# Moving bias adds, residual adds and PSUM evictions from VectorE to TensorE and ScalarE in a graph network kernel

## The chip, the cores and the metric

The kernel runs on one core of a Trainium2 chip. A core has TensorE (PE in the profile, with its weight loads listed apart as PEld), VectorE (DVE), ScalarE (ACT), GpSimd (POOL), and SyncE (SP), which issues DMAs here. Each engine executes its own instructions in program order, and engines wait for each other through semaphores. The metric is the time of one execution on the device in microseconds (us). The kernel before took 5338.34 us, the median of four runs that lie between 5337.52 and 5340.61 us.

## The reference

There are 16 graphs of 1024 nodes with 64 features each, and a weighted adjacency of 1024 x 1024 per graph. Four layers follow each other; each has the form x = layernorm(x + f(x, adj)).

```python
# layer 0
messages = einsum('bij,bjh->bih', adj, x)
f0 = tanh(concat([x, messages]) @ W1 + b1) @ W2 + b2
# layer 1
f1 = (adj / clip(sum(adj, axis=2), 1)) @ x
# layers 2 and 3, each with its own weights
adj_d = dilate(adj, mask)            # drops some neighbours of nodes with more than 10 of them
agg = 0.25*q(0.25) + 0.5*q(0.5) + 0.25*q(0.75)   # quantiles over each node's neighbours, per feature
f23 = (relu((x + agg) @ W1 + b1) @ W2 + b2) * mask
```

The quantiles need the neighbours' features in sorted order, for every node and feature. All arithmetic is float32 in and out.

## The kernel before

**Tiling.** A graph's features stand as eight tiles of 128 nodes x 64 features (NT = 8), and most steps work on halves of four tiles (G = 4, NH = 2). Nodes are ordered by their number of neighbours, so that tile t holds nodes with at most SIZES[t] of 10, 11, 13, 14, 15, 17, 19 and 33 members each. For tiles 0 to 6, POOL gathers the neighbours' rows from DRAM with indirect DMAs into a ring of ROOM slots in SBUF (`got_s`, line 352). For tile 7, with the longest lists, TensorE picks the rows by matmuls with one-hot matrices: VectorE writes a one-hot tile `hot` for each list position, and 24 matmuls (line 348) take the features, split into three bf16 parts, into PSUM (`pgk`), from where ScalarE copies them to `got` (line 727). The generator `fill` does this, 32 positions for each of two graphs, with `HOTS` = 4 buffers for `hot`. VectorE then sorts every list by a network of minima and maxima (`other`, `got_s`, `got`), ScalarE weighs the wanted order statistics (`weigh`, line 737), and VectorE sums them into `agg`.

**Rounds.** The main loop runs `sort_round(k)` for 18 rounds. Round k sorts layer 2 of graph k together with layer 3 of graph k-2. It sorts tiles 6 to 0, then calls `weave.finish(filling)`, which emits what is left of `fill`, and then sorts tile 7.

**The order of the work.** Everything besides the sorting is written as generators: `features` (layers 0 and 1 of a graph), `lists` and `ordered` (neighbour lists and their order), `fill`, `weigh`, and `finish` (the two small matrix products and the layernorm of layers 2 and 3). A planner, `Weave`, interleaves them with the sorting. Its clock is VectorE's estimated work, which the wrapper `Metered` adds up at 0.13 us plus one element a lane per cycle of 960 MHz. A generator yields the number of us after which it is due again, and `catch_up`, called after each sorting instruction, runs those that are due. `finish` and `advance` skip the clock forward when there is no sorting left to emit. The program order on VectorE, ScalarE and TensorE is the order in which these generators are run. The DMA queues of SP and POOL are filled by the same code.

**What the change touches.**

- `features`, layer 0: two halves. For each, TensorE transposes the own features and multiplies with the adjacency (`px`, lines 416 and 420), applies W1 (line 429), ScalarE takes tanh, and TensorE applies W2 into `pd` (line 436). After `yield 10`, VectorE adds `pd` and the own features x_s into y. After both halves VectorE adds the bias row b02r, which had been broadcast to 128 partitions. Then `settle` does the layernorm.
- `features`, layer 1: two halves. TensorE multiplies the adjacency with x1 and a column of ones (`pa`, line 451); VectorE makes the degree's reciprocal and multiplies `pa` by it into y. After both halves VectorE adds x1, and `settle` follows. Both `px`, `pd` and `pa` share one PSUM buffer (tag "x"). The flag `e.near`, for which `lists` polls, is set behind the second half.
- `finish`: VectorE adds the features xc to `agg`. For each half, TensorE transposes `agg` into `pt` (line 758), ScalarE copies it out, TensorE applies W1 (`ph`, line 764), ScalarE takes relu, and TensorE applies W2 into `pd` (line 771). After `yield 9` VectorE adds `pd` and the broadcast bias. After both halves VectorE multiplies by the mask, adds xc, and `settle` follows. `pt`, `ph` and `pd` share one PSUM buffer (tag "m").
- A second path for lists that are too long for the rounds (`layer0`, `layer1`, `mlp` at the end of the file) lies in a branch that these inputs do not take.

## Time and profile before

| | |
|---|---|
| median of four runs | 5338.34 us |
| the profiled execution's own time | 5337.5 us |
| its span, first to last instruction | 5335.7 us |
| mean granted TensorE clock | 0.732 |
| DVE busy | 4689.2 us in 9407 instructions |
| PE busy / PEld busy | 3428.3 us / 2656.0 us |
| POOL busy | 3658.9 us in 3228 instructions |
| ACT busy | 1969.3 us in 4644 instructions |

A row such as "L348 PE MATMUL pgk<-x3p,hot 128*128 128x64 bf16 x12288 | 597.7, 218 | 320.3 <-DVE hot L207 302.5" names the line, engine and operation, what is written from what, the shape and the count. Then come the busy time of the whole group, the mean ns of one instruction, and the idle time of the engine just before such instructions with what ended it. Line 207 is the wrapper through which every VectorE instruction of the rounds passes, so its instructions are told apart by their tiles. An f32 matmul with ordinary weights leaves two records, an f32 transpose leaves one: the 128 matmuls of line 436 are 256 records.

### The profile page before, as it was taken

What the parts mean: (1) busy time and instruction counts of PE and PEld (TensorE: products, weight loads), DVE (VectorE), ACT (ScalarE), POOL (GpSimd) and SP (SyncE); (2) the same over time, 40 slices, a digit from 0 to 9 for tenths busy, and PEclk for the clock granted to TensorE, in tenths of its full rate; (3) what the DMA queues carried; (4) which work ended last, traced back from release to release, by engine and by line L of the source; (5) the groups of instructions that cost most, each with busy time, mean ns of one, the idle gap of its engine ahead of it and who ended that gap; (6) DMA issues with size and microseconds to landing.
All of it is one profiled execution on the core that took longest, in us unless ns stands there. A gap on an engine that the chain in (4) does not pass through costs nothing.

```text
span 5335.7 us, 106955 instructions
## 1 busy us (share of the span) xinstructions
PE 3428.3 (64%) x43073; PEld 2656.0 (50%) x43144; DVE 4689.2 (88%) x9407; ACT 1969.3 (37%) x4644; POOL 3658.9 (69%) x3228
## 2 busy tenths in 40 slices
PE   6766477667585857858584867748576774625332
PEld 5645355455373645646363655636364563524222
DVE  2685779998999999999999989899898989999977
ACT  3351435243443525352524335342533534212111
POOL 0426547777678787787777776777678776787572
PEclk7877688678686968777787868777786866656555
DMA  3312122212122222222121222212122220111010
GB/s 87 76 39 60 31 59 58 69 42 55 41 59 57 58 57 56 60 54 61 37 73 35 50 58 52 63 40 70 31 50 58 54 48 18 28 22 26 15 24 10
DMA packets 420585, 259.11 MB, mean 49 GB/s; under 512 B 106590, under 2 KB 368878, under 8 KB 420078
## 3 DMA queue, kind: packets, MB, share of 16 engines
q0 software_dynamic: 102400, 105.06, 10.6%
q1 hardware_dynamic: 317678, 147.12, 10.0%
q8 instruction: 339, 5.55, 0.4%
q14 instruction: 168, 1.38, 0.1%
HBM read 239.37 MB, written 12.58 MB: 47 GB/s over the span
## 4 chain that ended last, share of the span: by engine, by line
DVE 66%; PE 14%; issue 8%; POOL 5%; DMA 3%; ACT 3%; SPq 0%; DVEq 0%; POOLq 0%; ACTq 0%
DVE other L207 21%; DVE got_s L207 15%; DVE got L207 9%; DVE hot L207 5%; POOL got_s L352 4%; DVE best L207 4%; PE pgk L348 4%; PE pk L592 3%; DMA got_s<-table,idx 3%; PE pa L451 2%; DVE less L207 2%; PE px L420 2%; DVE y_x L207 1%; PE pr L506 1%; DVE y_m L207 1%
## 5 line engine op out<-in xcount | busy, mean ns | idle before, releaser
L352 POOL DMA_INDIRECT got_s<-table,idx x2944 | 3363.7, 1143 | 1470.3 <-issue 775.1
L348 PEld LDWEIGHTS <-hot 128*128 128x128 bf16 x24576 | 1025.0, 112 | 707.3 <-DVE hot L207 629.5
L348 PE MATMUL pgk<-x3p,hot 128*128 128x64 bf16 x12288 | 597.7, 218 | 320.3 <-DVE hot L207 302.5
L348 PE MATMUL pgk<-x2p,hot 128*128 128x64 bf16 x12288 | 531.6, 208 | 228.1 <-DVE hot L207 219.5
L207 DVE TENSOR_TENSOR other<-got_s 128x512 f32<-128x512 f32 (+8 forms) x900 | 515.1, 584 | 47.4 <-DMA got_s<-table,idx 35.1
L737 ACT ACTIVATE got_s<-got_s,wts 128x64 f32<-128x64 f32 x1568 | 399.6, 335 | 355.5 <-DVE got_s L207 354.7
L207 DVE TENSOR_TENSOR got_s<-got_s 128x384 f32<-128x384 f32 (+7 forms) x918 | 491.1, 537 | 18.8
L207 DVE TENSOR_SCALAR hot<-place 128x1024 bf16<-128x1024 f16 x1024 | 448.5, 440 | 45.6 <-PE pgk L348 45.1
L592 PE MATMUL pk<-near,order 128*128 128x512 f16 x2048 | 475.4, 386 | 13.4 <-DVE order L207 8.0
L549 PE MATMUL pv<-minus_n,takes 128*128 128x128 bf16 x1024 | 230.6, 253 | 385.7 <-DVE takes L207 385.2
L506 PE MATMUL pr<-steps,near 128*128 128x512 bf16 x1465 | 382.6, 413 | 129.5 <-ACT junk L512 87.2
L451 PE MATMUL pa<-x,adj_r 128*128 128x65 f32 x2048 | 395.7, 375 | 92.0 <-DMA adj_r<-in_adj_dram 32.2
L451 PEld LDWEIGHTS pa<-x,adj_r 128*128 128x128 f32 x2048 | 383.2, 289 | 96.6 <-issue 37.8
L207 DVE TENSOR_TENSOR got_s<-other 128x512 f32<-128x512 f32 (+8 forms) x774 | 409.1, 541 | 7.2
L549 PEld LDWEIGHTS <-takes 128*128 128x128 bf16 x1024 | 116.0, 113 | 558.8 <-DVE takes L207 409.1
L207 DVE TENSOR_TENSOR other<-other 128x128 f32<-128x128 f32 (+13 forms) x558 | 318.8, 571 | 14.8
L548 PE MATMUL pv<-scaled,near 128*128 128x128 f16 x1024 | 231.5, 254 | 146.3 <-ACT near L553 146.2
L207 DVE TENSOR_TENSOR other<-got 128x128 f32<-128x128 f32 (+5 forms) x270 | 233.3, 881 | 103.6 <-ACT got L727 101.1
L506 PEld LDWEIGHTS <-near 128*128 128x128 f16 x1536 | 157.3, 105 | 328.3 <-issue 192.6
L592 PEld LDWEIGHTS <-order 128*128 128x128 bf16 x2048 | 195.7, 99 | 243.7 <-issue 23.3
L512 ACT ACTIVATE junk<-pr,nb_st 128x1024 f16<-128x1024 f32 x256 | 282.2, 1109 | 25.7 <-PE pr L506 25.0
L420 PE MATMUL px<-adj_r,x_s 128*64 128x128 f32 x2048 | 283.8, 299 | 10.6 <-DMA adj_r<-in_adj_dram 7.0
(195 smaller groups left out, 6268.4 us busy)
## 6 DMA issues: line engine op xcount, KB each, us to landing
adj_r<-in_adj_dram SPq DMA_DIRECT2D x256, 512.0 KB
got_s<-table,idx POOLq DMA_INDIRECT x2944
x_s<-in_x_dram SPq DMA_DIRECT2D x16, 256.0 KB
table<-x SPq DMA_DIRECT2D x16, 256.0 KB
x<-table SPq DMA_DIRECT2D x16, 256.0 KB
table<-x3s,rows POOLq DMA_INDIRECT x128
out_dram<-agg,out_rows POOLq DMA_INDIRECT x128
table<-no_row SPq DMA_DIRECT2D x6, 0.2 KB
```

What stands on the lines that cost most here:

```text
L207: return call(*args, **kwargs)
L348: nc.tensor.matmul(dst, hot[:, c, :], parts[:, c, q, :], start=first and c + q == 0, stop=c == NT - 1 and q == 2)
L352: nc.gpsimd.indirect_dma_start(out=dst, out_offset=None, in_=tab, in_offset=bass.IndirectOffsetOnAxis(ap=rows, axis=0))
L420: nc.tensor.matmul(px[C:, q * P : (q + 1) * P], x_s[:, jt, :], adj[t][:, jt, :], start=jt == 0, stop=jt == NT - 1)
L451: nc.tensor.matmul(pa[:, q, :], adj[i][:, jt, :], x1[:, jt, :], start=jt == 0, stop=jt == NT - 1)
L506: nc.tensor.matmul(pr[:, h * HALF : (h + 1) * HALF], near[:, c, t * P : (t + 1) * P], steps[:, ONSET + h * HALF - c * P :][:, :HALF], star ...
L512: nc.scalar.activation(junk, prs[t - 1], AF.Sign, bias=lim[:, i, t - 1 : t], scale=-1.0, accum_out=cut_at[:, i, t - 1 : t])
L548: nc.tensor.matmul(pv[:, cols], near[:, c, rows], scaled[:, c, :], start=True, stop=False)
L549: nc.tensor.matmul(pv[:, cols], takes[:, c, rows], minus_n, start=False, stop=False)
L592: nc.tensor.matmul(cols, order[:, c, t * P : (t + 1) * P], left(c, slice(h * G, (h + 1) * G)), start=c == 0, stop=c == NT - 1)
L737: nc.scalar.activation(prods[:, m, i, :], got[:, m, slot_id, :], AF.Copy, scale=e.wts[:, t, i : i + 1])
```

## The change

In layer 0, two more f32 matmuls follow each W2 matmul into the same PSUM columns: a one-row matmul of ones with the bias row, and the identity with the own features. ScalarE copies the finished sum to y. In layer 1, ScalarE takes `pa` out tile by tile with the reciprocal degree as its per-partition scale. In `finish`, xc and `agg` are both multiplied with the identity into `pt`, which adds and transposes them, the bias comes by a one-row matmul, and ScalarE takes `pd` out tile by tile with the mask as its scale. The broadcast bias tiles are replaced by three one-row tiles and a row of ones; the ring of gathered rows has 75 slots in place of 76. Several yields of the planner are added. The second path makes its own broadcast of the bias.

```diff
-ROOM = 76
+ROOM = 75
...
-    w01s, b01c, w02s, b02r = weight(w01, "w01s"), column(b01, "b01c"), weight(w02, "w02s"), per_row(b02, "b02r")
+    w01s, b01c, w02s = weight(w01, "w01s"), column(b01, "b01c"), weight(w02, "w02s")
...
+    bias_rows = [row(b, f"bias_row{i}") for i, b in enumerate((b02, b22, b32))]
+    ones_row = const.tile([1, P], F32, name="ones_row")
+    nc.vector.memset(ones_row, 1.0)
...
# features, layer 0
             for q in range(G):
-                nc.tensor.matmul(pd[:, q, :], hid_t[:, q * P : (q + 1) * P], w02s, start=True, stop=True)
+                nc.tensor.matmul(pd[:, q, :], hid_t[:, q * P : (q + 1) * P], w02s, start=True, stop=False)
+                nc.tensor.matmul(pd[:, q, :], ones_row, bias_rows[0], start=False, stop=False)
+                nc.tensor.matmul(pd[:, q, :], ident, x_s[:, h * G + q, :], start=False, stop=True)
             yield 10
-            dve.tensor_add(y[:, h * G : (h + 1) * G], pd, x_s[:, h * G : (h + 1) * G])
-        dve.tensor_add(y, y, b02r[:, None, :].to_broadcast([P, NT, C]))
+            nc.scalar.copy(y[:, h * G : (h + 1) * G], pd)
+        yield 4
...
# features, layer 1
-            dve.tensor_mul(y[:, h * G : (h + 1) * G], pa[:, :, :C], deg[:, 1, :, None].to_broadcast([P, G, C]))
+            yield 1
+            for q in range(G):
+                nc.scalar.activation(y[:, h * G + q, :], pa[:, q, :C], AF.Copy, scale=deg[:, 1, q : q + 1])
+        yield 5
         e.near = near
...
# finish
-        dve.tensor_add(agg, agg, xc)
         for h in range(NH):
             pt = s.psum.tile([P, HALF], F32, name="pt", tag="m", bufs=1)
             for q in range(G):
-                nc.tensor.transpose(pt[:C, q * P : (q + 1) * P], agg[:, h * G + q, :], ident)
+                nc.tensor.matmul(pt[:C, q * P : (q + 1) * P], xc[:, h * G + q, :], ident, start=True, stop=False)
+                nc.tensor.matmul(pt[:C, q * P : (q + 1) * P], agg[:, h * G + q, :], ident, start=False, stop=True)
...
             for q in range(G):
-                nc.tensor.matmul(pd[:, q, :], h_t[:, q * P : (q + 1) * P], w2s, start=True, stop=True)
+                nc.tensor.matmul(pd[:, q, :], h_t[:, q * P : (q + 1) * P], w2s, start=True, stop=False)
+                nc.tensor.matmul(pd[:, q, :], ones_row, bias_rows[1 + layer], start=False, stop=True)
             yield 9
-            dve.tensor_add(y[:, h * G : (h + 1) * G], pd, b2r[:, None, :].to_broadcast([P, G, C]))
-        dve.tensor_mul(y, y, e.mask[:, :, None].to_broadcast([P, NT, C]))
+            for t in range(h * G, (h + 1) * G):
+                nc.scalar.activation(y[:, t, :], pd[:, t - h * G, :], AF.Copy, scale=e.mask[:, t : t + 1])
+        yield 4
         dve.tensor_add(y, y, xc)
```

## The prediction

> **What bounds the kernel now.** I read the page's busy shares first, then the waits of VectorE, then one round in stretches, then VectorE's timeline where that round's fill ends.
>
> ```profile
> PE 3428.3 (64%) x43073; PEld 2656.0 (50%) x43144; DVE 4689.2 (88%) x9407; ACT 1969.3 (37%) x4644; POOL 3658.9 (69%) x3228
> ...
> DVE 66%; PE 14%; issue 8%; POOL 5%; DMA 3%; ACT 3%; SPq 0%; DVEq 0%; POOLq 0%; ACTq 0%
> ```
>
> VectorE is the busiest engine and holds two thirds of the chain that ended last. Its 646 us of idle time lie mostly at the start: it is busy 449 of the first 750 us.
>
> ```profile
> DVE other L207 <- ACT got L727: 101.1, 14, 10.7
> DVE y_x L207 <- PE pd L436: 58.5, 5, 20.0
> DVE hot L207 <- PE pgk L348: 45.1, 38, 4.3
> ```
>
> These are VectorE's three longest waits (total, times, longest). The second, which the change touches, falls in the first 750 us whole. The first comes once a round, where tile 7's sort waits for the last copy of the fill. One late round has these stretches (busy PE, PEld, DVE, ACT, POOL, then the granted clock):
>
> ```profile
> 3246.00:3300.00 54.00, 43.46 (x594) 33.88 (x595) 52.92 (x115) 25.69 (x61) 42.47 (x37) 0.81 0.27 61
> 3300.00:3350.00 50.00, 48.81 (x704) 33.27 (x702) 47.00 (x81) 18.92 (x36) 38.12 (x40) 1.00 0.21 49
> 3350.00:3400.00 50.00, 35.38 (x369) 32.30 (x370) 46.99 (x112) 8.48 (x27) 39.34 (x36) 0.56 0.30 67
> 3400.00:3452.00 52.00, 39.95 (x617) 33.94 (x617) 50.15 (x121) 14.88 (x51) 40.42 (x39) 0.70 0.35 80
> 3452.00:3555.00 103.00, 46.51 (x408) 33.74 (x411) 90.34 (x123) 56.05 (x119) 79.20 (x61) 0.70 0.13 30
> ```
>
> The round is 309 us: 206 us in which the 64 one-hot tiles of the fill are written amid the other work, then tile 7's sort. Everything that the change removes from VectorE lies in the first 206 us. PE is busy 167.6 of these, and 98% of the stretch from 3300. The end of the fill, on VectorE:
>
> ```profile
> 3448.23 0.28 DVE L207 TENSOR_TENSOR got_s<-got_s,other 128x128 f32<-128x128 f32 x1
> 3448.43 1.01 DVE L207 TENSOR_TENSOR got_s<-got_s 128x384 f32<-128x384 f32 x2
> 3449.47 0.29 DVE L207 TENSOR_TENSOR agg<-got_s 128x128 f32<-128x128 f32 x1
> 3449.68 0.76 DVE L207 TENSOR_SCALAR hot<-place 128x1024 bf16<-128x1024 f16 x2
> 3450.35 0.69 DVE L207 TENSOR_TENSOR y_x<-y_x,x2p 128x512 f32<-128x512 f32 x1
> 3450.95 1.34 DVE L207 TENSOR_SCALAR hot<-place 128x1024 bf16<-128x1024 f16 x3
> 3463.01 0.29 DVE L207 TENSOR_TENSOR other<-got 128x128 f32<-128x128 f32 x1 [10.72 <-ACT got L727]
> ```
>
> The sorting of tiles 6 to 0 has run out, five one-hot tiles are still to write, and then VectorE waits 10.7 us. So the fill's pace ends this stretch, not VectorE's work alone. Eleven rounds in a row, from 1078 us on, end so, with the last of that sorting 3 to 32 us before the last one-hot tile. This decides what removed VectorE work is worth.
>
> **What VectorE loses.** From the rows by shape: y_x<-pd,x_s 13.4 us (x32), y_x<-y_x,b02r 11.1 (x16), y_x<-pa,deg 13.6 (x32), agg<-agg with x2s and x3s 11.1 + 10.9 (x16 each), y_m<-pd with both biases 13.4 + 13.3 (x32 each), y_m<-y_m,mask_s 22.2 (x32). The sum is 109.0 us, 6.8 us for each of 16 graphs.
>
> **What that is worth in a round.** If VectorE alone set the round, 6.8 us. If the fill does, the sorting runs out 6.8 us sooner with 6.8/3.2 = 2.1 more one-hot tiles unwritten (206 us/64 = 3.2 us each while work runs beside them). These then go at the generator's own 2.1 us, which saves 2.1 x 1.1 = 2.3 us. I take 3.5, near the lower end, because the timeline shows the fill last; the rest above 2.3 is that fewer instructions delay the fill's due times. Eleven such rounds give 38 us. The round before them, where the sorting ended 0.3 us before the last one-hot tile, gives 6.8, and the last three, with only `finish` left (4.2 us), about 5 together: 12 us.
>
> **Where the 10.7 us wait moves.** Six rounds wait 9.0 to 10.7 us. In the one shown, TensorE does three groups of 11 matmuls of line 506 (2.75 us each) between the last one-hot tiles. Those belong to `lists`, which polls for e.near. The change adds 4 + 1 + 1 + 5 = 11 us of yields ahead of it and takes out 2.2 us of VectorE work, so these groups come about 9 us later, near the fill's end. Rounds without them waited 3.4 us. At best six rounds gain 7 us (42); at worst other work lands there and nothing is gained. I take 10.
>
> **What TensorE gains.** 384 bias matmuls and 128 identity matmuls into `pd`. No f32 matmul of one row is in the trace: the bound below is line 722's 0.207 us (92.7 us/448), above line 771's dearer half at 0.427 us (54.6 us/128); line 436, nearest in shape, has 45.6 us/128 = 0.356. 512 x 0.36 = 184 us (106 to 219). `pt` goes from 256 transposes (53.7 us) to 512 f32 matmuls of the shape of line 420 (283.8 us/1024 = 0.277), 142 us: 88 more. Together 272 us, 17 a graph, which lifts PE in the 206 us from 167.6 to about 185, 90%. Four buffers of `hot` cover most: the fills wait about 2 us a round on them. Where PE is 98% busy that cover is used up (hot at 3300.93 and 3303.75 waits already), and some 7 us of the new work lies ahead of 3306. If all of it arrived in VectorE it would cost 7 us a round, if the idle pieces before 3282 take it, nothing; I take 16 us over the run, 1.1 a round over 14 rounds.
>
> The clock for this work is read from the stretches: 1.00 at 98% PE busy, 0.56 at 71%. "TensorE: Matmul & The Clock Gate", Part 1 of the Trainium skill, says that activity releases the throttle and idling restores it, so more matmuls would not slow the others; the stretches fit that. By that page alone I would halve the 16 us; I keep it, since the 98% stretch was at full clock already.
>
> **What ScalarE gains.** 384 evictions of 128x64. Twelve such instructions of line 737 in a row took 2.97 us, 0.248 us each: 95 us. The 32 copies of 128x256 lie between that and line 761's 0.573 us for twice the columns; 0.36 gives 11 us. ScalarE would go from 37% to 39%, and its slack covers it. The Trainium skill speaks against the small pieces: "VectorE: DVE Perf Modes", the section on the TRN2 errata, gives ScalarE from PSUM 172 cycles plus the elements at 1.2 GHz and advises 512 or more elements. By it, as an estimate, a piece of 64 costs 197 ns and 96 undivided pieces of 256 would take 34 us where 384 small ones take 76. The row says 248, a little worse; either way the engine has room.
>
> **The new waits.** VectorE's add of `pd` used to come 6 to 10 us after the last matmul in layer 0 in the middle of the run, in `finish` 0.4 to 11 us. Now ScalarE waits there, with weighing and fill copies queued behind it, and VectorE's next use is 4 us (5 in layer 1) later. That covers bias matmuls (1.1 us a half at full clock) and 1.0 us of eviction except where slack was 0.4 us: about 1 us a round, inside the 16. TensorE's next half now waits for ScalarE in place of VectorE, in the single buffers "x" and "m"; its one-hot work queues behind.
>
> **The ends, where nothing covers latency.** First graph: 8 more matmuls a half (2.2 us at 0.278, from line 436's 8 records in 1.11 us), less the bias add of 0.69, and 0.6 plus a handover a half in layer 1: 6 us; the next two graphs, partly behind an adjacency DMA (31.4 us waited at 517): 2. So 8 (0 to 17). The last `finish`, from 5300: at the low clock there a half gets 1.9 (8 matmuls at 0.37 for 1.06), 1.5 (4 biases) and 0.7 us (four pieces at 0.248 and a handover against 0.42), 8.2 for two, less 1.4 for the adds removed: 7. The finish before it, ahead of queued output DMAs: 2. So 9 (4 to 15).
>
> **Costs nothing.** The bias loads (three on SP's queue before and after). ROOM 75: the ring's pieces end at 70 at most, by SIZES, so every place stays. POOL's gathers: its ring waits are 10 to 23 us in two rounds, so POOL could carry rounds 5 to 11 us shorter; if VectorE gained more than that, POOL would bind.
>
> **Sum** against the profiled 5337.5 us (0.8 below the median): -38 - 12 - 10 + 16 + 8 + 9 = -27, so 5310 us.
>
> **Rivals.**
> 1. VectorE sets the rounds after all: the whole 109 goes, with 20 more from the wait's move, less 17 at the ends and 16 for TensorE: 5337 - 96 = 5241 (5220 to 5285). For it: 93.7% busy from 890 to 4790 us (3652.9 of 3900). Against it: the five late tiles.
> 2. The gain is eaten within the round: the fill's pace returns only 2.3 us a round (25 over eleven), the other 12, against 33 of costs: -4, 5334 (5327 to 5348).
> 3. Slower: TensorE becomes the bound in the stretch that was 98% busy, and the 7 us of new work ahead of 3306 reach VectorE as waits of `hot`: 14 x 5.5 = 77 in place of 16, so -60 + 77 + 17 = +34, 5371 (5348 to 5410). It decides from 3.8 us of new wait a round, where -60 + 17 + 14 x 3.8 passes +11. Against it: the idle pieces of 2.3, 1.2 and 1.3 us before 3282 and the 70 to 77% after 3350.
>
> **Numbers.** Forecast 0.38 (5285 to 5327), rival 1 0.19, rival 2 0.15, rival 3 0.28. The 0.2% that a measurement can tell is 11 us: faster 0.57, same 0.15, slower 0.28. The range leaves out about a tenth on each side: 5235 to 5380.
>
> **What would show it.** Right: VectorE busy near 4580, PE up by some 200 to 270, ACT by 100, more one-hot tiles after the last sorting, and a shorter wait for the fill's copy. Wrong: `hot` waiting for `pgk` far above 45 us (rival 3), new waits of y or ln_st for ScalarE of over 2 us a round, or rounds under 303 us (rival 1).

## The result and the profile after

The changed kernel takes 5348.3 us (median of 31 runs, 5328.9 to 5361.1) where the kernel before, run beside it on the same chips, takes 5339.4 us (51 runs). The ratio is 1.0013, with a 95% interval of 1.0008 to 1.0018: no change by the 0.2% that was set as the bound. The forecast was 5310 us, half a per cent faster; no gain came, and the time is 38 us above it. The range of 5235 to 5380 us holds the time.

The profiled execution took 5342.8 us, with a span of 5341.0 us and a mean granted clock of 0.750. From the page of the changed kernel, the busy time of each engine and the shares of the chain that ended last:

```profile
PE 3717.4 (70%) x44869; PEld 2881.7 (54%) x44936; DVE 4588.9 (86%) x9200; ACT 2053.5 (38%) x5056; POOL 3652.6 (68%) x3228
...
DVE 58%; PE 18%; issue 8%; POOL 7%; DMA 4%; ACT 3%; DVEq 0%; POOLq 0%; SPq 0%; ACTq 0%
```

The work moved as the change says: VectorE loses 100.3 us, TensorE gains 289 us, ScalarE 84 us. But the span grew by 5.3 us, so VectorE's idle time grew from 646 to 752 us. TensorE's share of the chain rose from 14% to 18%. VectorE's waits in the changed kernel (total, times, longest) show where the idle time went:

```profile
DVE hot L207 <- PE pgk L349: 83.7, 52, 5.3
DVE near L207 <- DMA adj_r<-in_adj_dram: 64.2, 6, 25.8
DVE other L207 <- ACT got L733: 57.9, 11, 14.4
DVE ln_st_x L207 <- ACT y_x L441: 52.9, 5, 44.0
```

The wait for the last copy of the fill (`other` for `got`) fell from 101.1 to 57.9 us. Against that, the wait of `hot` for TensorE rose from 45.1 to 83.7 us, and the wait for adjacency blocks from 42.9 to 64.2 us.

**Where in the run.** VectorE writes 64 one-hot tiles for each of sixteen fills, so the first tile of a fill marks the start of a round. This table is worked out from the starts of those instructions in the traces, one execution each, in us. Its three middle kernels are experiments of the next section, put here so that the path from the first row to the last can be followed. (The expectations call the second fill that of the third round.)

| kernel | up to the second fill | that round | eleven rounds | two rounds | rest | span |
|---|---|---|---|---|---|---|
| before | 769.7 | 308.4 | 3408.0 | 518.3 | 331.3 | 5335.7 |
| before with the four yields | 775.8 | 291.8 | 3365.1 | 521.9 | 333.4 | 5288.0 |
| that, with the extra matmuls on zeros | 823.1 | 291.7 | 3423.2 | 522.8 | 341.9 | 5402.7 |
| changed without the extra matmuls | 779.6 | 320.4 | 3316.3 | 529.8 | 325.1 | 5271.2 |
| changed | 806.9 | 311.8 | 3363.8 | 526.8 | 331.7 | 5341.0 |

A second trace of the yields alone, on another chip, agrees with the second row to 2.2 us in every column but those of the eleven rounds, where it has 3375.0 us, and of the span; a difference of 10 us there is within what one program shows.

Between the first and the last row the start loses 37 us, the round of the second fill 3 us, the eleven rounds gain 44 us, and the last two rounds lose 8.5 us. The eleven rounds are not alike: in the changed kernel they are 300, 316, 317, 323, 313, 306, 303, 297, 296, 303 and 291 us long, where before has 337, 302, 305, 306, 302 and then 306 to 310.

**The start, where the clock is half.** TensorE's timeline in the changed kernel, first graph, second half of layer 0 (start, us, then the instruction; in brackets the idle time before it):

```profile
49.33 0.43 PE L437 MATMUL pd<-w02s,hid_t 64*128 64x64 f32 x2 [0.77 <-ACT hid_t L433]
49.70 0.43 PE L438 MATMUL pd<-bias_row,ones_row 1*128 1x64 f32 x2
50.05 0.47 PE L439 MATMUL pd<-x_s,ident 128*128 128x64 f32 x2
50.46 0.69 PE L437 MATMUL pd<-w02s,hid_t 64*128 64x64 f32 x2
...
55.38 0.69 PE L439 MATMUL pd<-x_s,ident 128*128 128x64 f32 x2
```

The same four W2 matmuls alone are one row of the kernel before:

```profile
47.60 1.10 PE L436 MATMUL pd<-w02s,hid_t 64*128 64x64 f32 x8 [0.77 <-ACT hid_t L432]
```

A matmul every 0.36 us turns into one every 0.61 us at 50.46. The four W2 matmuls alone took 1.10 us in the kernel before, 0.28 each, so the mixed sequence is slower even ahead of that. Two stretches of the changed kernel (length, then busy PE, PEld, DVE, ACT and POOL, then the granted clock):

```profile
40.08:50.32 10.24, 8.07 (x61) 6.58 (x59) 0.00 (x0) 1.84 (x3) 0.00 (x0) 1.00 0.65 189
50.40:56.10 5.70, 5.67 (x19) 4.48 (x18) 0.00 (x0) 0.00 (x0) 0.00 (x0) 0.50 0.09 26
```

And two of the kernel before:

```profile
38.46:48.70 10.24, 8.07 (x62) 6.57 (x60) 0.00 (x0) 1.84 (x3) 0.00 (x0) 1.00 0.69 194
48.70:56.00 7.30, 1.08 (x5) 1.11 (x6) 5.39 (x11) 2.21 (x3) 0.00 (x0) 0.50 0.05 15
```

The granted clock went from 1.00 to 0.50, and VectorE did nothing meanwhile (0.00 busy): the half-graph's `pd` took 6.7 us instead of 1.1. The kernel before has the same fall, after 10.24 us with the same 8.07 us of TensorE work. There it comes at 48.70, where the W2 matmuls end, and TensorE has little to do behind it (1.08 of 7.30 us). So the change did not bring the fall about; its matmuls reach into it.

**A middle round, where `hot` waits.** VectorE in the changed kernel, in the round from 2373 to 2686 us:

```profile
2513.44 0.61 DVE L207 TENSOR_SCALAR hot<-place 128x1024 bf16<-128x1024 f16 x1
2517.98 0.43 DVE L207 TENSOR_SCALAR hot<-place 128x1024 bf16<-128x1024 f16 x1 [3.93 <-PE pgk L349]
...
2524.73 0.43 DVE L207 TENSOR_SCALAR hot<-place 128x1024 bf16<-128x1024 f16 x1 [5.33 <-PE pgk L349]
```

And TensorE at the same time:

```profile
2514.19 0.41 PE L777 MATMUL pd<-w32s,h_t 128*128 128x64 f32 x2
2514.53 0.43 PE L778 MATMUL pd<-bias_row,ones_row 1*128 1x64 f32 x2
...
2517.07 1.87 PE L349 MATMUL pgk<-x3p,hot 128*128 128x64 bf16 x48
2518.76 5.00 PE L598 MATMUL pk<-near,order 128*128 128x512 f16 x16
```

The W2 and bias matmuls of `finish` (eight rows, 2514.19 to 2517.14) stand in TensorE's order ahead of the gathers that free the one-hot buffers. Four of the eight are new. The longer wait, 5.33 us, has the 5.00 us of line 598 in front of it, which the kernel before also does, only at another place in the round.

### The profile page after: what moved, and what is told of

The parts are those of the page before. It is cut to its first block, busy times and chain, and to the rows that moved or that the text cites. A ratio compares the mean times of both kernels' runs of the same rounds, so it can differ in the third digit from the quotient of the medians.

```text
span 5341.0 us, 110787 instructions
## 1 busy us (share of the span) xinstructions
PE 3717.4 (70%) x44869; PEld 2881.7 (54%) x44936; DVE 4588.9 (86%) x9200; ACT 2053.5 (38%) x5056; POOL 3652.6 (68%) x3228
## 4 chain that ended last, share of the span: by engine, by line
DVE 58%; PE 18%; issue 8%; POOL 7%; DMA 4%; ACT 3%; DVEq 0%; POOLq 0%; SPq 0%; ACTq 0%
DVE other L207 19%; DVE got_s L207 14%; DVE got L207 8%; POOL got_s L353 6%; PE pgk L349 4%; DVE hot L207 4%; PE pk L598 4%; DVE best L207 3%; DMA got_s<-table,idx 3%; PE pa L454 2%; DVE less L207 2%; PE px L421 2%; PE ordered_x L349 1%; DVE near L207 1%; POOL out_dram L789 1%
## 5 line engine op out<-in xcount | busy, mean ns | idle before, releaser
L349 PEld LDWEIGHTS <-hot 128*128 128x128 bf16 x24576 | 969.1, 109 | 782.9 <-DVE hot L207 682.4
L349 PE MATMUL pgk<-x3p,hot 128*128 128x64 bf16 x12288 | 535.9, 209 | 277.5 <-DVE hot L207 253.5
L512 PE MATMUL pr<-steps,near 128*128 128x512 bf16 x1469 | 398.6, 426 | 257.0 <-ACT junk L518 154.3
L207 DVE TENSOR_SCALAR hot<-place 128x1024 bf16<-128x1024 f16 x1024 | 449.7, 441 | 84.5 <-PE pgk L349 83.7
L598 PE MATMUL pk<-near,order 128*128 128x512 f16 x2048 | 488.5, 395 | 17.4 <-DVE order L207 13.9
L555 PE MATMUL pv<-minus_n,takes 128*128 128x128 bf16 x1024 | 205.8, 237 | 198.1 <-DVE takes L207 195.9
L207 DVE TENSOR_TENSOR other<-got 128x128 f32<-128x128 f32 (+5 forms) x270 | 232.7, 881 | 60.6 <-ACT got L733 57.9
L421 PE MATMUL px<-adj_r,x_s 128*64 128x128 f32 x2048 | 270.2, 290 | 3.4 <-ACT node_in L424 2.9
L743 ACT ACTIVATE got<-got,wts 128x64 f32<-128x64 f32 x672 | 165.0, 336 | 265.7 <-DVE got L207 265.7
L421 PEld LDWEIGHTS px<-adj_r,x_s 128*64 128x64 f32 x2048 | 241.1, 146 | 22.0 <-issue 12.9
```

The lines of the kernel that those rows point to most:

```text
L207: return call(*args, **kwargs)
L349: nc.tensor.matmul(dst, hot[:, c, :], parts[:, c, q, :], start=first and c + q == 0, stop=c == NT - 1 and q == 2)
L421: nc.tensor.matmul(px[C:, q * P : (q + 1) * P], x_s[:, jt, :], adj[t][:, jt, :], start=jt == 0, stop=jt == NT - 1)
L512: nc.tensor.matmul(pr[:, h * HALF : (h + 1) * HALF], near[:, c, t * P : (t + 1) * P], steps[:, ONSET + h * HALF - c * P :][:, :HALF], star ...
L555: nc.tensor.matmul(pv[:, cols], takes[:, c, rows], minus_n, start=False, stop=False)
L598: nc.tensor.matmul(cols, order[:, c, t * P : (t + 1) * P], left(c, slice(h * G, (h + 1) * G)), start=c == 0, stop=c == NT - 1)
```

## The experiments

Three things came in one edit: more TensorE work, less VectorE work (with ScalarE taking the results), and four yields that move work in the program order. The runs take them apart. A letter that an expectation gives a theory is explained there. The comparisons belong to five groups of runs. In three of them the kernel before took 5336.6 to 5338.9 us; in the other two, on two other chips, it took 7470.8 and 7614.5 us, with TensorE stopping every few matmuls (the last section). Sizes are taken from the first three; the ratios of the other two are given where they add something. The kernels d, g, m1, i and v have a ring of 70 slots in place of 75 or 76. By the kernel's rule for placing lists in the ring, every list lies in the same slots with all three sizes, so the ring is no cause of a difference.

### The four yields, taken away and alone

```diff
# a_no_yields: the changed kernel
             nc.scalar.copy(y[:, h * G : (h + 1) * G], pd)
-        yield 4
...
-            yield 1
...
-        yield 5
         e.near = near
...
-        yield 4
         dve.tensor_add(y, y, xc)
```

> The changed kernel without the planner's four added yields (4 in layer 0, 1 and 5 in layer 1, 4 in finish). Theory Y (the yields delay each graph's preparation: in the changed kernel the third round's fill starts at 807 us instead of 770, and the next graphs' lists then fall into the fills): that fill starts at about 785, the rounds from 1418 to 2686 (316, 317, 323, 313 us) fall back to about 305, and the kernel takes 5290 to 5310 us. Theory P (the extra f32 matmuls on TensorE and the handover to ScalarE do it): the start stays at 800 or more and the time within 10 us of 5341.

```diff
# c_yields_alone and c_second: the kernel before
+        yield 4
         dve.tensor_add(y, y, b02r[:, None, :].to_broadcast([P, NT, C]))
...
+            yield 1
             dve.tensor_mul(y[:, h * G : (h + 1) * G], pa[:, :, :C], deg[:, 1, :, None].to_broadcast([P, G, C]))
+        yield 5
         e.near = near
...
+        yield 4
         dve.tensor_mul(y, y, e.mask[:, :, None].to_broadcast([P, NT, C]))
```

> The kernel before with the four yields at the same places and nothing else of the change. Theory Y: the third round's fill starts 15 us or more later than 770 us, and the kernel is 20 to 60 us slower than before. Theory P: the fill starts within 5 us of 770 and the time is within 10 us of before.

> The kernel before with the four yields alone; the same program as c_yields_alone, as the base of this call. If the gain of 0.85% lies in where the planner places the lists beside the fill, it comes again on a chip where the kernel before takes 5340 us: 5290 to 5300 us; where TensorE waits for its own instruction stream it may be anything between 1% faster and 1% slower.

Without the yields the changed kernel takes 5437.7 us, a ratio of 1.0187 (1.0170 to 1.0204). The kernel before with the yields takes 5296.0 us, 0.9915 (0.9898 to 0.9931), and on another chip 5290.2 us, 0.9906 (0.9890 to 0.9923). So the yields are worth 43 to 49 us by themselves, without any work moved to another engine, and about 1.7% to the changed kernel. Neither theory had this: Y expected the yields to cost time and P that they change nothing, and without them the second fill still starts late, at 805.7 us. Waits of the changed kernel without yields:

```profile
DVE other L207 <- ACT got L730: 95.1, 14, 12.1
DVE y_m L207 <- ACT y_m L778: 95.0, 21, 18.5
```

VectorE's add behind the last eviction of `finish` now comes at once: `y_m` waits 95.0 us where it waited 34.4 us with the yields. The wait for the fill's last copy is back at 95.1 us.

Waits of the kernel before with the yields:

```profile
DVE other L207 <- ACT got L730: 59.1, 12, 9.3
DVE y_m L207 <- PE pd L774: 47.0, 12, 12.3
DVE y_x L207 <- PE pd L436: 43.9, 6, 19.6
DVE hot L207 <- PE pgk L348: 43.3, 26, 5.4
```

The wait for `got` falls from 101.1 to 59.1 us, and to 67.9 us in the trace of the other chip: 33 to 42 of the 43 to 49 us. In the rounds from 3536 to 4433 us it is 3.5 us instead of 10.7. In the round before these, whose fill is last copied at 3439 us, it is 7.2 us; there the first group of list counting (line 506 of before, 509 here) starts only at 3444.33, behind the last one-hot tiles, which are written from 3429.14 on. That is the move that the prediction described.

### One part of the change at a time

`d_layer0_alone` keeps only layer 0's part of the change, with its yield; layer 1 and `finish` are as before. `g_no_layer0` is the reverse.

```diff
# d_layer0_alone: the changed kernel, for example in finish
-                nc.tensor.matmul(pt[:C, q * P : (q + 1) * P], xc[:, h * G + q, :], ident, start=True, stop=False)
-                nc.tensor.matmul(pt[:C, q * P : (q + 1) * P], agg[:, h * G + q, :], ident, start=False, stop=True)
+                nc.tensor.transpose(pt[:C, q * P : (q + 1) * P], agg[:, h * G + q, :], ident)
# g_no_layer0: the changed kernel, in layer 0
-                nc.tensor.matmul(pd[:, q, :], ones_row, bias_rows[0], start=False, stop=False)
-                nc.tensor.matmul(pd[:, q, :], ident, x_s[:, h * G + q, :], start=False, stop=True)
             yield 10
-            nc.scalar.copy(y[:, h * G : (h + 1) * G], pd)
-        yield 4
+            dve.tensor_add(y[:, h * G : (h + 1) * G], pd, x_s[:, h * G : (h + 1) * G])
+        dve.tensor_add(y, y, broadcast[0][:, None, :].to_broadcast([P, NT, C]))
```

> Only the layer 0 part of the change (bias and own features added by TensorE, one copy by ScalarE, yield 4); layer 1 and finish are as before. The ring has 70 slots, which are all that its pieces reach. Theory P with TensorE's extra f32 matmuls in the preparation as the cause: this part alone brings most of the 37 us at the start (fill at 795 or later), against 24.5 us of VectorE work removed. Theory Y: about 4/11 of the delay, fill at 780 to 785, time 5325 to 5345.

> The change without its layer 0 part: layer 1 and finish are changed, 84 us of VectorE work are removed, 256 bias matmuls and the double transposes are added. Theory P with the layer 0 matmuls as the cause: fill at 780 or sooner and a time of 5270 to 5300. Theory Y: fill at 790, time 5300 to 5330. If the finish matmuls crowd the fills, waits of hot for pgk stay above 70 us and the time stays near 5340.

Layer 0 alone: 5356.7 us, 1.0034 (1.0019 to 1.0048). All but layer 0: 5335.7 us, 0.9996 (0.9986 to 1.0006). The second fill starts at 797.0 us in the first and at 777.6 us in the second (before: 769.7), so the loss at the start belongs to layer 0. These starts are as theory P had them (795 or later, 780 or sooner), but the 5335.7 us are far above the 5270 to 5300 that it gave the second kernel. There `hot` waits 88.1 us for TensorE, which is above the 70 us that the expectation named as the sign of `finish`'s matmuls crowding the fills. The two parts bring +0.34% and -0.04%, and the whole +0.13%: they do not add up exactly, which the layer 1 and stacked runs below show again.

### The extra matmuls without the handover, and the handover without the matmuls

These two are the core of the study. The first adds to the kernel before the four yields and all the extra matmuls, but on zeros, while VectorE and ScalarE keep their work. The second is the changed kernel without any of the extra matmuls; its sums lack the bias rows, layer 0's own features and `finish`'s xc in `pt`.

```diff
# m1: the kernel before with the four yields, layer 0 and finish
-                nc.tensor.matmul(pd[:, q, :], hid_t[:, q * P : (q + 1) * P], w02s, start=True, stop=True)
+                nc.tensor.matmul(pd[:, q, :], hid_t[:, q * P : (q + 1) * P], w02s, start=True, stop=False)
+                nc.tensor.matmul(pd[:, q, :], ones_row, zeros[:1, :], start=False, stop=False)
+                nc.tensor.matmul(pd[:, q, :], ident, zeros, start=False, stop=True)
...
-                nc.tensor.transpose(pt[:C, q * P : (q + 1) * P], agg[:, h * G + q, :], ident)
+                nc.tensor.matmul(pt[:C, q * P : (q + 1) * P], zeros, ident, start=True, stop=False)
+                nc.tensor.matmul(pt[:C, q * P : (q + 1) * P], agg[:, h * G + q, :], ident, start=False, stop=True)
...
-                nc.tensor.matmul(pd[:, q, :], h_t[:, q * P : (q + 1) * P], w2s, start=True, stop=True)
+                nc.tensor.matmul(pd[:, q, :], h_t[:, q * P : (q + 1) * P], w2s, start=True, stop=False)
+                nc.tensor.matmul(pd[:, q, :], ones_row, zeros[:1, :], start=False, stop=True)
# m2: the changed kernel
-                nc.tensor.matmul(pd[:, q, :], ones_row, bias_rows[0], start=False, stop=False)
-                nc.tensor.matmul(pd[:, q, :], ident, x_s[:, h * G + q, :], start=False, stop=True)
...
-                nc.tensor.matmul(pt[:C, q * P : (q + 1) * P], xc[:, h * G + q, :], ident, start=True, stop=False)
-                nc.tensor.matmul(pt[:C, q * P : (q + 1) * P], agg[:, h * G + q, :], ident, start=False, stop=True)
+                nc.tensor.transpose(pt[:C, q * P : (q + 1) * P], agg[:, h * G + q, :], ident)
...
-                nc.tensor.matmul(pd[:, q, :], ones_row, bias_rows[1 + layer], start=False, stop=True)
```

> The kernel before with the four yields and with all the extra f32 matmuls of the change, which here add zeros; VectorE keeps its adds, its bias rows and its evictions, so nothing is taken from it. Against the yields alone (5296 us). Theory M (TensorE's extra matmuls are what the change pays): 5360 to 5400 us, the third round's fill at 795 or later in place of 777. Theory H (the handover to ScalarE and VectorE's waits for it are what it pays): 5296 to 5315 us, fill at 777 to 783.

> The changed kernel without its extra matmuls: ScalarE takes everything out of PSUM and the yields stay, but the biases of layers 0, 2 and 3, the own features in layer 0 and xc in the input of finish are left out of the computation. Theory M: 5230 to 5270 us, below the yields alone at 5296 by what 109 us less VectorE work is worth, and fill at 777 or sooner. Theory H: 5320 to 5345 us, fill near 800.

> The kernel before with the four yields and all the extra f32 matmuls adding zeros, VectorE as before; the same program as m1_yields_matmuls, for a chip on which the kernel before takes some 5340 us. [...] Theory M (TensorE's extra matmuls are what the change pays): 5360 to 5400 us. Theory H (the handover to ScalarE is): 5296 to 5315 us.

> The changed kernel without its extra matmuls (biases of layers 0, 2 and 3, own features in layer 0 and xc in the input of finish are left out of the computation); the same program as m2_no_matmuls, for a chip on which the kernel before takes some 5340 us. Theory M: 5230 to 5270 us, third round's fill at 777 or sooner. Theory H: 5320 to 5345 us, fill near 800.

> The kernel before with the four yields and all the extra f32 matmuls adding zeros, VectorE as before; the same program as m1_yields_matmuls, beside the yields alone on the same chip. Theory M: 1.2 to 2% slower than the yields alone (on a chip where the kernel before takes 5340 us: 5360 to 5400 us against 5296). Theory H: within 0.4% of the yields alone.

> The changed kernel without its extra matmuls (biases of layers 0, 2 and 3, own features in layer 0 and xc in the input of finish are left out of the computation); the same program as m2_no_matmuls, beside the yields alone on the same chip. Theory M: faster than the yields alone by 0.5 to 1.2% (5230 to 5270 us where the kernel before takes 5340). Theory H: slower than the yields alone by 0.4% or more.

On the two chips where TensorE stops, the first gave 1.0284 (1.0259 to 1.0308) and 1.0267 (1.0243 to 1.0292), the second 0.9925 (0.9902 to 0.9949) and 0.9869 (0.9849 to 0.9890). The third time, beside `c_second` on a chip where the kernel before takes 5338.7 us, the matmuls on zeros gave 5404.2 us, 1.0119 (1.0102 to 1.0136), and the changed kernel without them 5267.1 us, 0.9864 (0.9848 to 0.9881).

Theory M was right in direction, and its sizes were not quite met: 5404.2 us lie 2.2% above the yields alone, where 1.2 to 2% were expected, and 5267.1 us 0.4% below them, where it was 0.5 to 1.2%.

So the extra matmuls cost 114 us on top of the yields (5404.2 less 5290.2), though VectorE and ScalarE do the same work. On top of the changed kernel's handover they cost 80 us by the ratios (1.0013 less 0.9864, of 5339) and 69.8 us by the two spans. The page of each kernel gives the busy times; the yields alone, the yields with the matmuls, and the changed kernel without the matmuls, in this order:

```profile
PE 3376.7 (64%) x43144; PEld 2588.4 (49%) x43144; DVE 4681.6 (89%) x9407; ACT 1963.2 (37%) x4640; POOL 3677.6 (70%) x3228
```

```profile
PE 3728.0 (69%) x44936; PEld 2872.8 (53%) x44936; DVE 4682.4 (87%) x9409; ACT 1962.7 (36%) x4640; POOL 3670.9 (68%) x3228
```

```profile
PE 3374.2 (64%) x43144; PEld 2599.0 (49%) x43144; DVE 4585.5 (87%) x9200; ACT 2055.2 (39%) x5056; POOL 3666.4 (70%) x3228
```

The matmuls add 351 us of TensorE work in the one pair and 343 us in the other; the +289 us of the result's page is smaller because the yields alone took 52 us off TensorE's busy time. How they reach VectorE is seen in the waits of the kernel with the matmuls on zeros, beside those of the yields alone above:

```profile
DVE y_m L207 <- PE pd L782: 104.3, 17, 21.3
DVE y_x L207 <- PE pd L442: 87.0, 10, 24.1
...
DVE hot L207 <- PE pgk L352: 55.5, 33, 5.4
```

The wait of `y_m` for `pd` goes up by 57.3 us, that of `y_x` for `pd` by 43.1 us, that of `hot` by 12.2 us. These are 112.6 of the 114 us; nine tenths of the rise are waits for `pd`, and one tenth is a shortage of one-hot buffers. In layer 0 the longer wait for `pd` is the matmuls' own length, as one half shows; first TensorE and VectorE with the yields alone, then with the matmuls on zeros:

```profile
151.50 1.97 PE L436 MATMUL pd<-w02s,hid_t 64*128 64x64 f32 x8 [3.29 <-ACT hid_t L432]
153.51 0.42 DVE L207 TENSOR_TENSOR y_x<-pd,x_s 128x256 f32<-128x256 f32 x1 [7.62 <-PE pd L436]
```

```profile
161.89 0.69 PE L440 MATMUL pd<-w02s,hid_t 64*128 64x64 f32 x2 [3.29 <-ACT hid_t L436]
...
168.66 0.69 PE L442 MATMUL pd<-zeros,ident 128*128 128x64 f32 x2
169.39 0.42 DVE L207 TENSOR_TENSOR y_x<-pd,x_s 128x256 f32<-128x256 f32 x1 [13.11 <-PE pd L442]
```

The matmuls of this half take 7.46 us instead of 1.97, and VectorE waits 13.11 us instead of 7.62: both grow by 5.49. In the five other halves of the first 800 us in which VectorE waits in both kernels the two growths agree to 0.2 us. For `y_m` that is only a part: at its longest wait the matmuls into `pd` grow from 1.00 to 2.87 us, and the wait from 12.3 to 21.3 us, with TensorE's longer work for `pt` and layer 0 ahead of it; the rest was not taken apart. The waits are not spread like the loss. Outside the eleven rounds those for `pd` rise by 74.6 us, where 56.6 us are lost (other waits shrink, that for adjacency blocks by 9.9 us); in the eleven rounds they make 25.8 of 58 us. By the table, 47 us of it lie ahead of the second fill, 58 us in the eleven rounds (5.3 a round), and 8.5 us from the last fill on. The extra matmuls did not move the planned order: the place of `lists` beside the fill, measured below, is the same to 0.1 us in the late rounds with and without them, in both pairs.

The handover by itself, with the yields already there, brings 23 us (5290.2 less 5267.1), though VectorE does 96 us less. Here is where the rest went, by the table: the eleven rounds gain 48.8 us (4.4 a round), the end 8 us, but the round of the second fill loses 28.6 us, the start 4 us and the last two rounds 8 us. Waits of VectorE in that kernel, from 770 to 1110 us:

```profile
DVE near L207 <- DMA adj_r<-in_adj_dram: 30.2, 1, 30.2
```

With the yields alone no such wait falls there. SP's queue shows what comes late; first with the yields alone, then the changed kernel without the matmuls:

```profile
828.66 0.37 SPq L468 DMA_DIRECT2D table<-x  x1
836.15 0.37 SPq L323 DMA_DIRECT2D x_s<-in_x_dram  x1
911.80 174.36 SPq L403 DMA_DIRECT2D adj_r<-in_adj_dram  x16
```

```profile
866.48 0.37 SPq L469 DMA_DIRECT2D table<-x  x1
873.84 0.37 SPq L324 DMA_DIRECT2D x_s<-in_x_dram  x1
947.78 158.31 SPq L404 DMA_DIRECT2D adj_r<-in_adj_dram  x13
```

The store of a graph's layer 1 result into the table goes out 38 us later, the load of the next graph's features stands behind it on the queue, and the adjacency blocks come 36 us later. The same wait is in the changed kernel (21.7 us), and in `g_no_layer0`, `d_layer0_alone`, `j_second` and `v_stacked` (25.2, 24.7, 27.6 and 30.1 us). The traces agree on the store: counted from the second fill's start it goes out after 75 to 87 us in these six kernels, and after 45 to 53 us in before, both runs of the yields alone, `i_second`, the matmuls on zeros and the changed kernel without yields, where that wait is 3.0 us at most. So in these traces the wait comes only where yields stand together with the handover of layer 0 or of `finish`; layer 1's handover alone does not bring it. An experiment that moves the store alone was not made.

### Which matmuls cost

```diff
# j: the changed kernel without layer 0's extra matmuls
-                nc.tensor.matmul(pd[:, q, :], hid_t[:, q * P : (q + 1) * P], w02s, start=True, stop=False)
-                nc.tensor.matmul(pd[:, q, :], ones_row, bias_rows[0], start=False, stop=False)
-                nc.tensor.matmul(pd[:, q, :], ident, x_s[:, h * G + q, :], start=False, stop=True)
+                nc.tensor.matmul(pd[:, q, :], hid_t[:, q * P : (q + 1) * P], w02s, start=True, stop=True)
```

> The changed kernel without layer 0's extra matmuls (its bias and own features are left out of the computation); the copy by ScalarE and the rest stay. Theory M: the first fill starts at 223 to 227 us in place of 238, the third round's at 780 in place of 807, and the time is 5300 to 5325. Theory H: fills within 4 us of the changed kernel's, and 5335 to 5348 us.

> The changed kernel without layer 0's extra matmuls (its bias and own features are left out of the computation); the same program as j_no_layer0_matmuls, for a chip on which the kernel before takes some 5340 us. If layer 0's matmuls make most of the price at the start, the third round's fill starts at 785 or sooner in place of 807, the time is 0.990 to 0.995 of before, and what is left above the kernel without any extra matmul (0.9864) is the price of those in finish. If they do not, 0.997 or more.

5302.6 us, 0.9933 (0.9916 to 0.9949); on a chip where TensorE stops 1.0082 (1.0059 to 1.0104). Against the changed kernel's 1.0013, layer 0's 256 matmuls cost 0.8%, 43 us; against the 0.9864 without any, those of `finish` cost 0.7%, 37 us. The second fill starts at 783.5 us without layer 0's and at 806.9 us with them.

### Less VectorE work, without extra matmuls

`h` leaves out two things that the change takes from VectorE, layer 0's bias row and the mask, and nothing takes their place. `i` is the kernel before with the yields and with layer 1 taken out of PSUM by ScalarE, which needs no matmul.

```diff
# h: the kernel before
-        dve.tensor_add(y, y, b02r[:, None, :].to_broadcast([P, NT, C]))
...
-        dve.tensor_mul(y, y, e.mask[:, :, None].to_broadcast([P, NT, C]))
# i: the kernel before with the four yields
-            dve.tensor_mul(y[:, h * G : (h + 1) * G], pa[:, :, :C], deg[:, 1, :, None].to_broadcast([P, G, C]))
+            for q in range(G):
+                nc.scalar.activation(y[:, h * G + q, :], pa[:, q, :C], AF.Copy, scale=deg[:, 1, q : q + 1])
```

> The kernel before without two of VectorE's instructions, the add of layer 0's bias row and the multiplication by the mask, 33 us in all, which are left out of the computation; no yield and nothing on another engine is changed. It measures what less VectorE work is worth by itself. If VectorE sets the rounds: 5305 us. If the fill sets them, as the prediction took it (half of the work returned): 5320 us. If the order of the work that comes out of the planner counts for more than either: outside 5300 to 5340.

> The kernel before without VectorE's add of layer 0's bias row and its multiplication by the mask, 33 us, left out of the computation; the same program as h_drop_adds, for a chip on which the kernel before takes some 5340 us. If VectorE sets the rounds: 5305 us. If the fill sets them and returns half: 5320 us. If the order out of the planner counts for more than either: outside 5300 to 5340 (the other chip gave 0.7% slower).

> The yields and the layer 1 part of the change alone: ScalarE takes the layer 1 sums out of PSUM, which needs no matmul more, layer 0 and finish are as before but for their yields. Theory M: this part costs TensorE nothing, so 13.6 us of VectorE work go at no price: 5280 to 5296 us, below the yields alone. Theory H: 5300 to 5315 us.

> The yields and the layer 1 part alone; the same program as i_yields_layer1, for a chip on which the kernel before takes some 5340 us. Theory M: 0.988 to 0.992 of before, 13.6 us of VectorE work gone at no price. Theory H: 0.994 or more.

`h` ran only on the two chips where TensorE stops: 1.0067 (1.0041 to 1.0094) and 1.0029 (0.9997 to 1.0062). What dropped VectorE work alone is worth on the other chips stays open. `i` gave 1.0048 (1.0033 to 1.0063) there, and 5313.8 us, 0.9957 (0.9941 to 0.9974), on a chip where before takes 5336.6 us. That is faster than before, but slower than the yields alone (0.9906 and 0.9915), with 10.5 us less VectorE work (4671.1 against 4681.6) and no matmul added. The loss lies in the eleven rounds (3386.9 us, against 3365.1 and 3375.0 in the two traces of the yields alone).

The last one was built to beat both: yields, layer 1 by ScalarE, and layer 0's own features and bias stacked with the hidden features into one operand of 128 rows, so that one matmul does all three.

```diff
# v_stacked: the changed kernel with finish as before (and its yield)
+    own_w02 = const.tile([P, C], F32, name="own_w02")
+    nc.sync.dma_start(own_w02[C:], w02)
+    nc.vector.tensor_copy(own_w02[:C], ident[:C, :C])
...
-                    nc.scalar.copy(node_in[:C], px[:C])
+                    nc.scalar.activation(node_in[:C], px[:C], AF.Identity, bias=b02c)
...
-            nc.scalar.activation(hid_t, px[:C], AF.Tanh, bias=b01c)
+            nc.scalar.activation(node_in[C:], px[C:], AF.Tanh, bias=b01h[C:])
...
-                nc.tensor.matmul(pd[:, q, :], hid_t[:, q * P : (q + 1) * P], w02s, start=True, stop=False)
-                nc.tensor.matmul(pd[:, q, :], ones_row, bias_rows[0], start=False, stop=False)
-                nc.tensor.matmul(pd[:, q, :], ident, x_s[:, h * G + q, :], start=False, stop=True)
+                nc.tensor.matmul(pd[:, q, :], node_in[:, q * P : (q + 1) * P], own_w02, start=True, stop=True)
```

> A version without extra matmuls: the yields, layer 1 by ScalarE, and in layer 0 the own features plus the bias stay in the upper half of the same 128-row operand as tanh's result, with the identity stacked over W2, so that one matmul of the old count gives the whole sum and ScalarE copies it out; finish is as before but for its yield. VectorE loses 38 us. Theory M (the extra matmuls are what the change pays): below the yields alone (0.9906 to 0.9915 of before), 0.985 to 0.990. Theory H: 0.992 or more. On a chip where TensorE waits for its instruction stream no verdict.

It takes 5336.1 us, 0.9999 (0.9990 to 1.0009): no gain. Both `i` and this kernel came out where theory H had them (0.994 or more, 0.992 or more) and not where theory M had them: without any extra matmul, less VectorE work still brought nothing over the yields alone. So the matmuls are not all that the change pays for. The longest waits of `v_stacked`:

```profile
DVE hot L207 <- PE pgk L364: 97.1, 50, 5.0
DVE near L207 <- DMA adj_r<-in_adj_dram: 77.1, 5, 35.5
```

VectorE does 27.5 us less than with the yields alone, yet the wait of `hot` more than doubles (43.3 to 97.1 us), and the round of the second fill has the adjacency wait of 30.1 us. The likely reason is where the work of `lists` stands against the fill. I measured it as the time from a round's first one-hot tile to the next graph's first `takes` instruction in the late rounds: -56 us in the kernel before (rounds of 309 to 310 us), +2 with the yields alone (299 to 302), +11 to +15 in `i` (299 to 304), +11 in `v_stacked` (300 to 309), +1 falling to -31 in the changed kernel without the matmuls (289 to 299), -51 to -57 without yields (312 to 318). These edits of VectorE's work also moved this place, and no run moved it alone. At the same +11 the rounds differ by up to 9 us, so the place alone does not set them. So this is argued, not shown.

**The version to keep** is the kernel before with the four yields: 5290 to 5296 us, 0.9906 to 0.9915 of the time, faster than both kernels of this study.

## Why the prediction was right or wrong

The path by the spans is: yields -47.7, then the handover -16.8, then the matmuls +69.8, together +5.3 us. In the other order the matmuls are +114.7 and the handover -61.7. The prediction had -10 for what moves, -50 for VectorE in the rounds, and 33 for TensorE and the ends. What failed is the 33: TensorE's extra matmuls cost 70 to 115 us, which used up a gain of 64.5 us by the spans, about the 60 that were forecast.

**What VectorE loses: right.** 109.0 us was worked out; the page shows 100.3, and 96.1 with equal yields. ScalarE has 84 us more where 106 were worked out. The 384 small evictions took 88.7 us of ScalarE, 0.23 each, where 0.25 was taken. That its slack covers this holds for the eleven rounds, where `best` waits 4.7 us for ScalarE's `code`; over the whole run that wait rose from 21.9 to 50.2 us, while the yields alone have 19.7: 9 more (29.1) come without the matmuls and 21 with them. Two readings on VectorE were slightly off and change little: of its 646 us of idle time 301 lie in the first 750 us, not most, and by the rows `finish` loses 4.4 us a graph and layers 0 and 1 lose 2.4, where 4.2 and 2.2 were used.

**What that is worth in a round: nearly right in the eleven rounds, wrong in the others.** 3.5 us a round were taken; 4.4 (without the matmuls) and 5.4 (with them) were measured. That is more than the half that was assumed, of the 6.0 us that VectorE really lost (96.1 over 16 graphs). How far it is the fill that sets these rounds stays open, since the place of `lists` moved too. The 12 us for the remaining rounds failed: the round of the second fill lost 28.6 us, with the adjacency wait behind SP's queue, and the two last ones lost 8, where one wait for gathered rows took 15.3 us instead of 3.1. That is the limit the prediction had named, that POOL's gathers would bind if the rounds got shorter. The step named SP's queue for the bias loads only, and not for the stores and loads that the moved layers issue.

**Where the wait moves: mechanism right, size too small.** It was priced at 10 us between 0 and 42, and is the largest gain of the change: the yields alone bring 43 to 49 us, and that wait gets 33 to 42 us shorter. I chose a value near the lower end because other work could have landed there; the trace of before already showed rounds with 3.4 us, and this is what most of the last rounds became. Seven of the eleven rounds waited 9.0 us or more, not six.

**What TensorE gains: this step failed.** The work was sized at 272 us and is 343 to 351 us. A one-row f32 matmul costs about what a full one does: line 778's 256 bias matmuls are 129.3 us, 0.51 us each, and layer 0's 128 full identity matmuls are 69.2 us, 0.54 each, where 0.36 was taken. In the timeline of the start both kinds come every 0.36 us at the granted 0.99 and every 0.61 at 0.50, so 0.36 is the price at full clock. Its price in the rounds, 16 us, is 36 us with the handover (4202.4 less 4166.5, the three middle columns) and 59 us without. What failed with it is the sentence on the new waits, that the 4 us to VectorE's next use cover the new latency except for about 1 us a round. In the eleven rounds VectorE's waits with the matmuls on zeros are

```profile
DVE hot L207 <- PE pgk L352: 39.9, 19, 5.4
DVE y_m L207 <- PE pd L782: 23.8, 10, 2.8
DVE place L207 <- PE pp L675: 8.3, 5, 2.5
DVE y_x L207 <- PE pd L442: 5.0, 2, 3.4
```

and with the yields alone

```profile
DVE hot L207 <- PE pgk L348: 27.1, 13, 5.4
DVE y_m L207 <- PE pd L774: 3.0, 5, 0.8
```

`y_m` waits 20.8 us more, `hot` 12.8, `place` at least 7 and `y_x` 5: together 46 of the 58 us. Four bias matmuls at 0.36 are 1.4 us a half at full clock, where the slack was as low as 0.4 us.

**The ends: this step failed too.** The start was priced at 8 us, at most 17, and is 37. Of that the yields are 6, the handover 4 and the matmuls 27. They were counted at full clock, 2.2 us a half; at the granted 0.50 a half took 6.7 us against 1.1, 5.6 more. The rule that was weighed, "TensorE: Matmul & The Clock Gate", Part 1 of the Trainium skill, says that idling brings the throttle back. From it the prediction took that more matmuls would not slow the others. The start does not agree: TensorE was busy for 8.07 of the 10.24 us ahead of the fall, with no idle time over 0.77 us, and the clock fell all the same. In the kernel before it stayed at 0.50 from 56.00 to 89.60 us, where TensorE was busy for 32.38 of 33.60 us. What sets the clock there stays open. The last stretch was priced at 9 and is 0.4 in sum; the matmuls alone are 6.6 to 8.5 there, near the price, and the handover without them gives 8 back.

**The rivals.** The time lies at the edge between rival 2 (up to 5348) and rival 3 (from 5348). Rival 2 said that the fill gives back too little of VectorE's gain; that is a part of it, with 17 of 96 us returned in the comparison without the matmuls, but by another way (the adjacency wait and `hot`), and the eleven rounds returned more than predicted. Rival 3 said that TensorE's work reaches VectorE as waits of `hot`. The size is near it, 69.8 to 114.7 us, but the way is another: with the matmuls on zeros the waits for `pd` rise by 100 us, and `hot` by 12.2. In the changed kernel, where ScalarE stands between, adding the matmuls raises `ln_st_x` by 19.3 us (33.6 to 52.9), `y_m` by 14.0 (20.4 to 34.4), `best` by 21.1 and `hot` by 13.8. Rival 1 is out for the whole run: of the 96 us, 17 came through without the matmuls and 62 with them. The sign to watch, `hot` far above 45 us, came true at 83.7, yet without the matmuls it is already 69.9; so this sign did not tell the rival apart.

**Open** are the worth of VectorE work dropped alone on an ordinary chip, the part that the place of `lists` has in the difference between the yields alone, `i` and `v_stacked`, which of the four yields bring the gain, and why the store of layer 1's result goes out later.

## What to carry to other kernels

Before handing adds from VectorE to TensorE, look for the instruction that waits for the PSUM result and how far behind it stands: here matmuls that fitted into TensorE's idle time cost 70 to 115 us, because most of the longer waits in the cleanest comparison were for the results of these matmuls, on a chain that VectorE waited for. Price such matmuls by the granted clock of the very stretch and of what follows it, since in the first graph the new ones ran into a fall to 0.50, and price a one-row matmul as a full one. When an edit carries along small changes of order, run these alone first: here they gained 43 to 49 us, and the work that was moved gave all of it back.

## What the runs showed of the hardware that was not expected

The kernel before takes 5337 to 5339 us on three chips and 7470.8 and 7614.5 us on two others. On the latter TensorE's longest idle time stands under "issue", in which it waits for nothing that the profile shows. TensorE's timeline in the changed kernel without the matmuls, on the chip with 7470.8 us:

```profile
4026.19 0.33 PE L349 MATMUL pgk<-x2p,hot 128*128 128x64 bf16 x3 [0.49 <-issue]
4026.92 0.33 PE L349 MATMUL pgk<-x2p,hot 128*128 128x64 bf16 x3 [0.40 <-issue]
4027.63 0.43 PE L349 MATMUL pgk<-x2p,hot 128*128 128x64 bf16 x5 [0.38 <-issue]
```

The one-hot matmuls stop for 0.4 to 0.5 us after every three to five, 1123.4 us in line 349 together, while VectorE's 128x512 minima take 0.69 us as everywhere. There the 1792 more records of the matmuls on zeros, with the yields, made the kernel 2.7 to 2.8% slower instead of 1.2%. Why these chips differ no trace shows. The expectations call it waiting for TensorE's own instruction stream; the DMA queue of the instructions gives no sign of that, since for the changed kernel without the matmuls it moves the same 339 packets on both kinds of chip, in 0.4% of the engines' time on one and 0.3% on the other.

The granted clock can fall to half in the midst of steady work: the stretch from 50.40 to 56.10 us is 99% busy at 0.50, right behind 10.24 us at 1.00 and 79% busy. The kernel before shows the same fall at 48.70 us.
